# A second GRN product by 38 block products on quarters of the positions in place of 15 on halves

## The chip, the core and the metric

The kernel runs on one core of a Trainium2 chip. The metric is the device time of one execution in microseconds (us). Three runs of the kernel before gave 3122.0, 3122.22 and 3123.13 us; the median is 3122.22. The profile comes from one further execution.

## The reference

The input is 32 images of 384 channels and 28 x 28 = 784 positions, in fp32. A ConvNeXt block with global response normalization is followed by a gate; everything is computed in fp32.

```python
y = depthwise_conv7x7(x) + dw_b                  # per channel
y = layernorm over channels(y) * ln_g + ln_b     # per position
y = gelu(y @ w1 + b1)                            # 384 -> 1536 features
gx = sqrt(sum over positions(y**2))              # per image and feature
y = grn_g * (y * gx / (mean(gx) + eps)) + grn_b + y
x = x + (y @ w2 + b2)                            # 1536 -> 384
avg, mx, mn = mean, max, min of x over the positions
logits = concat(avg @ W1.T, (W2_1 . mx per group) * W2_2, mn @ W3.T) @ Wfc.T
out = sigmoid(logits[:, :, None, None] + x)
```

The change concerns `y @ w2`. For one image it is a product of a 384 x 1536 matrix (the weights) with a 1536 x 784 matrix (the features by positions).

## The kernel before

**Stages.** Until about 484 us the depthwise convolution runs for all images, as matmuls with banded matrices (lines 529 to 533); its result goes to memory (`yd`, `yl`). In the same stretch GpSimd makes the sums of weight blocks that the later products need (`form_w`, lines 448 to 456) and stores them (`u1d`, `u2d`). Then each image has two stages. `up(b)` (line 752) is the first product with GELU, `down(b)` (line 837) the second product with the residual. The order is up(0), up(1), down(0), up(2), down(1), and so on. In mid-run one image takes 81.75 us: for instance a first product starts at 1437.94, the second one at 1477.44 and the next first product at 1519.69 us.

**Both products use a fast block algorithm.** A 3 x 3 by 3 x 2 block product takes 18 block multiplications in the ordinary way. Here it takes 15: each multiplies a sum of weight blocks (made once, ahead) by a sum of input blocks (a "form", made per image), and the results are added to and subtracted from the output blocks. In the second product, the 1536 features are split in three groups by k = 0 to 2 (each of KT = 4 blocks of 128 partitions), and the 784 positions in two halves "a" and "b" of NH = 392. `FORMS` lists the ten sums of inputs, `STEPS` the fifteen products:

```python
    ("s", None, "r", "2a", ALU.subtract),     # FORMS: s = r - 2a
    ("r", "+02-20+21", "B", 0, "+2a"),        # STEPS: input r, weights, bank, first, reads
```

A step loads its summed weights (256 KB, `u2d[i]`, SyncE's DMA queue, six buffers in turn), multiplies four times on TensorE into its bank (line 859; an fp32 matmul is two records in the trace, so a step is eight records of 392 columns), and then VectorE reads the bank into the output `xt`, which holds the residual (lines 873 and 875). An output block and half is read two to four times. The last read of each (line 875) also adds b2 and sums over the positions; once both halves of a block are final, two reductions over 784 positions give its maximum and minimum (line 882).

**The forms** are made by GpSimd, each as one instruction over 4 x 392 = 1568 elements per partition (line 834): seven (`EARLY`) are issued during the preceding first product, three within the second. Six places (`SLOTS`) hold them; some take the place of an input block that is no longer needed. The same ten forms over 392 elements are made for the first product's input (`forms_up`, line 246, instructions of line 269).

**The order around it** is written out by hand as hooks: `within(b)` (line 936) hangs work onto the steps of the first product, `beside(b)` (line 977) onto those of the second. In `within(b)` stand the scaling of the previous image's features by 1 + g * nx (`scale`, line 812, ScalarE), its forms, and half of this image's GELU and squares. In `beside(b)`, where n = b + 1, stand: the transposes of image b+2's normalized input on TensorE and their copies out (`turn`, `evac`), `forms_up(b+2)` at step 4, the input of image b+3 (`load_y`, line 202) at step 3 and its statistics (`stats`, line 208) at step 8, the rest of image n's GELU and squares, its GRN factor (`grn`, line 794), the gate of image b-1 (`gate_store`, line 888) and the load of image n's residual (`load_x`) at step 10. The gate multiplies 96 values of each partition on GpSimd (`zt`, line 894), sums them over partitions by one matmul (`pa`), and so on to the sigmoid.

A framework turns the hooks into one queue per engine; it may move an instruction ahead of others unless the code says `keep_in_program_order`. PSUM has eight banks: seven go round in the pool `psz`, one (`pss`, "small") serves the two tiny matmuls of `grn` and the gate.

Of the kernel before, what the change touches and what calls it, by code (L numbers as in the profile page):

```python
# [56 lines left out]
    ("w", "1b", "0b", "1b", ALU.add),  # L57
# [4 lines left out]
    ("v", None, "u", "2a", ALU.subtract),  # L62
    ("x", "0a", "v", "w", ALU.subtract),
    ("z", "0b", "v", "2b", ALU.subtract),
)
UPFORMS = "pqrstuvwxz"
EARLY = 7
SLOTS = 6

STEPS = (
    ("0b", "+10-11", "G", 1, "-0b+1b"),
    ("0a", "+00", "D", 1, "-1a+0a"),
    ("p", "-20+21", "B", 1, "-2b"),
    ("s", "-02", "E", 1, "+0a"),
    ("r", "+02-20+21", "B", 0, "+2a"),
    ("2a", "-02+20+22", "E", 0, "+2a"),
    ("1a", "+01+20-21", "B", 0, "+0a"),
    ("t", "+00+10-11", "C", 1, "+0b"),  # L80
    ("x", "+20", "A", 1, "+2a"),
    ("u", "-00-10-12", "C", 0, "-1a"),
    ("v", "-12-20", "A", 0, "+1a"),
    ("w", "-11+20", "F", 1, "+1a-1b"),
    ("z", "+12", "A", 0, "-1b"),
    ("q", "+00-01-02+10-11", "B", 0, "-0b"),
    ("2b", "+12+20-21-22", "A", 0, "-2b"),
)
NS = len(STEPS)

# [18 lines left out]
)  # L109
KT = FB // 3  # L110
UG = 5
# [11 lines left out]
def convnext_gate_kernel(  # L123
# [20 lines left out]
    pss = ctx.enter_context(tc.tile_pool(name="pss", bufs=1, space=bass.MemoryType.PSUM))  # L144

    def small(name):
        return pss.tile([P, 512], F32, tag="small", name=name)

# [5 lines left out]
    u2d = dram.tile([NS, P, KT * P], F32, name="u2d")  # L154
# [14 lines left out]
    NQ = 4 * CB  # L169
# [30 lines left out]
    bss = {}  # L200

    def load_y(b):
        yi = yis[b] = yip.tile([P, NY, NJ, YC], F32, tag="yi", name=f"yi_{b}")
        yk = yi.rearrange("p k j c -> p k (j c)")
        nc.sync.dma_start(yk[:, : NY - NLAST], yd[:, :, b, :])
        nc.sync.dma_start(yk[:, NY - NLAST :], yl[:, :, b, :])

    def stats(b):

        mv = sts[b] = smp.tile([P, NJ, 2], F32, tag="mv", name=f"mv_{b}")  # L210
        if b == 0:
            bs = bss[0].rearrange("p j i v -> p j (i v)")
        else:
            bs = smp.tile([P, NJ, 6], F32, tag="bs", name=f"bs_{b}")
            for j in range(NJ):
                nc.vector.bn_stats(bs[:, j, :], yis[b][:, :, j, :])
        for j in range(NJ):
            nc.vector.bn_aggr(mv[:, j, :], bs[:, j, :])

# [26 lines left out]
    def forms_up(b, eng=nc.gpsimd):  # L246
# [6 lines left out]
        if b == 1:  # L253
            aft = [
                dp.tile([P, KT, NH], F32, tag="d", name=f"af_{b}_{i}") for i in range(-(-ns // KT))
            ]
            af = [aft[n // KT][:, n % KT, :] for n in range(ns)]
        else:
            af = [room_af[:, n, :] for n in range(ns)]
        byname = {f[0]: f for f in FORMS}  # L260
        n = 0
        for name in UPFORMS:
            _, place, in0, in1, op = byname[name]
            if name == "w":
# [4 lines left out]
            eng.tensor_tensor(d, o[in0], o[in1], op)  # L269
# [3 lines left out]
    with ExitStack() as one:  # L273
        tp = one.enter_context(tc.tile_pool(name="tp", bufs=1))
        xtp = one.enter_context(tc.tile_pool(name="xtp", bufs=2))
        ufp = one.enter_context(tc.tile_pool(name="ufp", bufs=2))
# [127 lines left out]
        w2v = ws.rearrange("p (t k m c) -> p t k m c", t=KT, k=3, c=P)  # L404
        U1, U2 = 4, 22
        stores = []
        SG = 40

        def gate_weights():

            for h in range(2):
                nc.vector.tensor_scalar(
                    gate[:, : 2 * CB, :].rearrange("p (cb h) r -> p h cb r", h=2)[:, h],
                    awt[:, 0], 1.0 / NT, None, ALU.mult,
                )
            nc.vector.tensor_copy(gate[:, 3 * CB :, :], awt[:, 1])
            for cb in range(CB):
# [10 lines left out]
                out=gate[:, 2 * CB : 3 * CB, :], in_=grp_a, pattern=[[-P, CB], [G, R]],  # L428
                compare_op=ALU.is_ge, fill=0.0, base=G - 1, channel_multiplier=-1,
            )  # L430
            pf = small("pf")
# [5 lines left out]
            for v in range(3):  # L437
                q0, nq = ((0, 2 * CB), (2 * CB, CB), (3 * CB, CB))[v]
# [9 lines left out]
        def form_w(name, wv, text, dst):  # L448

            t = ufp.tile([P, KT, P], F32, tag="uf", name=name)  # L450
# [102 lines left out]
        def store(yc, kt, b0, b1):  # L553
# [6 lines left out]
            if b0 == 0:  # L560
                for j in range(NJ):
                    nc.vector.bn_stats(bss[0][:, j, 1 + i, :], yc[:, 0, j, :])
# [53 lines left out]
        for s in range(NK):  # L616
# [37 lines left out]
            else:  # L654
# [4 lines left out]
                if s % 2:  # L659
                    store(yc, kt, 0, B)  # L660
                    if kt == NY - NLAST - 1:

                        yi = yis[0] = yip.tile([P, NY, NJ, YC], F32, tag="yi", name="yi_0")
                        nc.sync.dma_start(
                            yi[:, : NY - NLAST].rearrange("p k j c -> p k (j c)"), yd[:, :, 0, :]
                        )
                        bs0 = bss[0] = smp.tile(
                            [P, NJ, 1 + NLAST, 6], F32, tag="bs0", name="bs0", bufs=1
                        )
                        for j in range(NJ):  # L670
                            nc.vector.bn_stats(bs0[:, j, 0, :], yi[:, : NY - NLAST, j, :])
# [13 lines left out]
            i = s - U2  # L685
            if 0 <= i < NS:
                form_w(f"u2_{i}", w2v, STEPS[i][1], u2d[i].rearrange("p (t c) -> p t c", c=P))

# [3 lines left out]
    u2_tiles = [up2.tile([P, KT * P], F32, name=f"u2_{i}") for i in range(5)]  # L692
    u2_tiles.append(ws[:, NU1 * UG * P : NU1 * UG * P + KT * P])
# [5 lines left out]
    dp = ctx.enter_context(tc.tile_pool(name="dp", bufs=SLOTS))  # L699
    psz = ctx.enter_context(tc.tile_pool(name="psz", bufs=7, space=bass.MemoryType.PSUM))  # L700
# [93 lines left out]
    def grn(b):  # L794
# [6 lines left out]
        pg = small(f"pg_{b}")  # L801
# [10 lines left out]
    def scale(b, f, eng=nc.scalar):  # L812
        y = ys[b][:, f, :]
        affine(eng, y, y, gscs[b][:, f : f + 1], gb_t[:, f : f + 1])

    def forms(b, n0, n1):
# [248 lines left out]
```

## Time and profile before

| what | value |
|---|---|
| median of three runs | 3122.22 us (3122.0 to 3123.13) |
| profiled execution, its own time | 3123.22 us |
| its span in the trace | 3121.5 us |
| granted TensorE clock, mean | 0.998 |
| ScalarE: GELU (line 744), one of 784 elements | 944 ns, 384 of them |
| VectorE: read of a bank of the first product (line 783), 392 elements | 562 ns |
| VectorE: maximum or minimum over 784 (line 882) | 964 ns, 192 of them |
| GpSimd: form for the first product (line 269), 392 elements | 1015 ns |
| GpSimd: the gate's input (line 894), 96 elements | 350 ns |
| SyncE DMA: weights of the first product, 320 KB | 3.0 us from issue to landing |
| DMA in all | 540.81 MB, mean 173 GB/s |

In a line of the groups, a name such as `pz_A<-y,u` is out<-in with the image's number left out, `128x392 f32` the tile (partitions x elements per partition), `x512` the number of instructions; then follow their busy time in us and the mean of one in ns, and last the idle time of the engine ahead of them with what ended most of it. Durations of matmul records overlap, so their pace is taken from starts. In a line of the timeline, the first number is the start and the second the length of a run of like instructions, both in us, the last `xN` how many there are; `[... <-...]` is the wait ahead of it.

### The profile page before, as it was taken

What the parts mean: (1) busy time and instruction counts of PE and PEld (TensorE: products, weight loads), DVE (VectorE), ACT (ScalarE), POOL (GpSimd) and SP (SyncE); (2) the same over time, 40 slices, a digit from 0 to 9 for tenths busy, and PEclk for the clock granted to TensorE, in tenths of its full rate; (3) what the DMA queues carried; (4) which work ended last, traced back from release to release, by engine and by line L of the source; (5) the groups of instructions that cost most, each with busy time, mean ns of one, the idle gap of its engine ahead of it and who ended that gap; (6) DMA issues with size and microseconds to landing.
All of it is one profiled execution on the core that took longest, in us unless ns stands there. A gap on an engine that the chain in (4) does not pass through costs nothing.

```text
span 3121.5 us, 34685 instructions
## 1 busy us (share of the span) xinstructions
PE 3097.7 (99%) x11555; PEld 2005.6 (64%) x11555; DVE 1683.8 (54%) x3452; ACT 1953.1 (63%) x3123; POOL 1542.5 (49%) x766
## 2 busy tenths in 40 slices
PE   8999999999999999999999999999999999999998
PEld 8999996555555555555555555555555555555554
DVE  3444436655555555555555555555555555555554
ACT  3333335767667677666667666676666766767762
POOL 1232301645555555555555555555555555555555
PEclk9999999999999999999999999999999999999999
DMA  9999976444444444444444444444444444444334
GB/s 366 367 369 352 351 289 202 133 127 133 146 146 144 146 146 144 135 141 146 142 147 142 149 142 150 142 146 145 143 138 138 133 146 147 144 145 146 126 107 130
DMA packets 294315, 540.81 MB, mean 173 GB/s; under 512 B 125151, under 2 KB 134906, under 8 KB 285178
## 3 DMA queue, kind: packets, MB, share of 16 engines
q1 hardware_dynamic: 281156, 499.80, 49.2%
q10 hardware_dynamic: 12982, 38.80, 3.4%
q8 instruction: 93, 1.52, 0.2%
q14 instruction: 84, 0.69, 0.1%
HBM read 447.53 MB, written 90.99 MB: 173 GB/s over the span
## 4 chain that ended last, share of the span: by engine, by line
PE 98%; DMA 1%; ACT 1%; DVE 0%; issue 0%; ACTq 0%; SPq 0%; POOLq 0%; DVEq 0%
PE ph_B L774 13%; PE ph_C L774 13%; PE ph_A L774 13%; PE pz_A L859 11%; PE pz_B L859 11%; PE pz_E L859 5%; PE pz_C L859 5%; PE pc L529 5%; PE pc L533 4%; PE pc L531 4%; PE pz_F L859 3%; PE pz_D L859 3%; PE pz_G L859 3%; PE py L732 2%; PE pt L386 2%; DMA dwb<-in_cvec 0%
## 5 line engine op out<-in xcount | busy, mean ns | idle before, releaser
L744 ACT ACTIVATE y<-y,fv 128x784 f32<-128x784 f32 x384 | 347.2, 944 | 194.3 <-DVE y L789 171.6
L774 PE MATMUL ph_B<-room,ws 128*128 128x392 f32 x1240 | 458.9, 492 | 1.5 <-DMA yi<-yl 1.5
L774 PE MATMUL ph_C<-room,ws 128*128 128x392 f32 x1240 | 459.0, 492 | 0.0
L774 PE MATMUL ph_A<-room,ws 128*128 128x392 f32 x1240 | 458.9, 492 | 0.0
L234 ACT ACTIVATE y<-y,fv,gsc 128x784 f32<-128x784 f32 x376 | 365.5, 1030 | 142.4 <-DVE gsc L810 142.4
L834 POOL TENSOR_TENSOR d_v<-d_u,y 128x1568 f32<-128x1568 f32 x32 | 112.7, 3523 | 588.5 <-PE pz_B L859 588.3
L774 PEld LDWEIGHTS ph_B<-room,ws 128*128 128x128 f32 x1240 | 235.4, 190 | 173.6 <-issue 1.8
L774 PEld LDWEIGHTS ph_A<-room,ws 128*128 128x128 f32 x1240 | 235.5, 190 | 172.8 <-ACT y L781 0.6
L774 PEld LDWEIGHTS ph_C<-room,ws 128*128 128x128 f32 x1240 | 235.3, 190 | 172.2 <-DVE y L787 0.4
L750 ACT ACTIVATE junk<-y 128x784 f32<-128x784 f32 x384 | 328.4, 855 | 6.9
L269 POOL TENSOR_TENSOR room<-room 128x392 f32<-128x392 f32 x300 | 294.3, 1015 | 2.3
L785 DVE TENSOR_TENSOR y<-y,ph_B 128x392 f32<-128x392 f32 x256 | 137.8, 559 | 206.0 <-ACT y L744 129.8
L894 POOL TENSOR_TENSOR zt<-gate,st 128x96 f32<-128x96 f32 x32 | 11.2, 350 | 460.4 <-PE ph_C L774 438.7
L783 DVE TENSOR_TENSOR y<-y,ph_C 128x392 f32<-128x392 f32 x384 | 215.7, 562 | 30.9
L834 POOL TENSOR_TENSOR y<-d_v,y 128x1568 f32<-128x1568 f32 x64 | 223.7, 3517 | 2.4
L545 ACT ACTIVATE yc<-pc,dwb 128x224 f32<-128x224 f32 (+1 forms) x200 | 103.4, 617 | 189.0 <-PE pc L533 180.5
L529 PE MATMUL pc<-xt,tmat 128*128 128x224 f32 (+1 forms) x800 | 213.8, 349 | 4.9 <-ACT xt L397 3.4
L533 PE MATMUL pc<-xt,tmat 128*128 128x192 f32 (+1 forms) x800 | 192.9, 323 | 0.0
L531 PE MATMUL pc<-xt,tmat 128*96 128x192 f32 (+1 forms) x800 | 191.1, 321 | 0.0
L395 DVE COPY xt<-pt 128x512 f32<-128x512 f32 (+1 forms) x184 | 112.0, 618 | 133.7 <-PE pt L386 133.6
L859 PE MATMUL pz_A<-y,u 128*128 128x392 f32 x512 | 179.0, 492 | 0.0
L882 DVE TENSOR_REDUCE st<-x 128x1 f32<-128x784 f32 x192 | 177.1, 964 | 3.3
(168 smaller groups left out, 5701.9 us busy)
## 6 DMA issues: line engine op xcount, KB each, us to landing
ws<-u1d SPq DMA_DIRECT2D x384, 320.0 KB, 3.0
u<-u2d SPq DMA_DIRECT2D x400, 256.0 KB, 2.7
tmat<-fs SPq DMA_DIRECT2D x47, 1420.0 KB, 11.7
yd<-yc SPq DMA_DIRECT2D x22, 1792.0 KB, 6.6
yi<-yd SPq DMA_DIRECT2D x32, 1232.0 KB, 6.9
x<-in_x SPq DMA_DIRECT2D x32, 1176.0 KB, 6.2
out<-x ACTq DMA_DIRECT2D x31, 1176.0 KB, 5.4
room<-in_x SPq DMA_DIRECT2D x84, 392.0 KB, 11.3
```

Of the source, the lines that this page charges most:

```text
L234: eng.activation(out, in_, AF.Identity, bias=add, scale=mul)
L269: eng.tensor_tensor(d, o[in0], o[in1], op)
L529: keep(nc.tensor.matmul(po, t[:, c, P : 2 * P], xc, start=True, stop=False))
L531: nc.tensor.matmul(lo, t[:, c, 2 * P : T0 + MW], after, start=False, stop=False)
L533: keep(nc.tensor.matmul(hi, t[:, c, :P], before, start=False, stop=True))
L744: nc.scalar.activation(y, y, AF.Gelu, bias=b1_t[:, f : f + 1], scale=1.0)
L750: nc.scalar.activation(junk, ys[b][:, f, :], AF.Square, accum_out=ssqs[b][:, f : f + 1])
L774: nc.tensor.matmul(banks[t, bk][:, :NH], wts[t][:, i % UG, :], o[opnd], start=(first == 1), stop=True, skip_group_check=True,)
L783: nc.vector.tensor_tensor(d, d, p, ALU.add)
L834: nc.gpsimd.tensor_tensor(d, o[in0], o[in1], op)
L859: nc.tensor.matmul(pz[:, :NH], wt[:, t, :], o[opnd][:, t, :], start=(first == 1 and t == 0), stop=(t == KT - 1), skip_group_check=True,)
L882: nc.vector.tensor_reduce(st[:, q : q + 1], xt[:, m, :], AX.X, op2)
```

## The change

The second product becomes a 4 x 3 by 4 x 4 block product: the features are split in four groups (KD = 3 blocks of 128 each), the weights' outputs in three as before, the positions in four quarters "a" to "d" of NQ4 = 196. In the ordinary way that is 48 block products; the new `STEPS` have 38, and `SUMS` has 39 sums of inputs of 3 x 196 = 588 elements per partition, some of which only serve further sums. A step is three matmuls of 196 columns. With it come:

- **Sums by need** (`sums(b)`, `used(b, name)`): GpSimd's sums are issued in the fixed order of `SUMS`, each as soon as its inputs are scaled and a place is free. There are 15 places of 588 elements; a place is freed after the last use, counted in program order. The call stands after every step and in the hooks of the first product. `forms_up` is issued when all sums are ("after sums").
- **Weights**: two steps' weights per load (`UD` = 2, 384 KB, 19 loads per image), five buffers. There are 38 weight sums to be made during the convolution, with 109 terms in place of 36.
- **Reads**: 51 in place of 18, of 196 columns. Twelve are final ones; each of these now has its own maximum and minimum over 196 positions at once, and three small reductions at the end join the quarters.
- **Order**: the features are scaled in the group order 1, 3, 2, 0, six blocks still in the second product and six in the first. The input of image b+1 is loaded at the start of up(b), with its issue behind the last weight load of the second product (`issue_after`); its statistics go into the second half of up(b)'s first pass (hooks (0, 20) to (0, 28)) one block at a time. The input of image 0 is loaded in two parts.
- **Banks**: the pool of the small matmuls is gone, `psz` has eight.
- **The end**: the gate of image b-1 hangs at step `part(11)` = 27 of down(b) in mid-run, at `part(9)` = 22 in down(30) and at step ND - 8 = 30 in down(31), the last one; the last image's sums are offered at every step of down(30) from `part(8)` = 20 on.

```diff
--- before.py
+++ after.py
-UPFORMS = "pqrstuvwxz"
-EARLY = 7
-SLOTS = 6
...
+SUMS = (
+    ("s0", "1b", "+", "1c"),
+    ("s1", "3c", "-", "2c"),
+    ("s2", "s0", "+", "s1"),
+    ("s3", "s2", "+", "3d"),
+    ("s4", "3c", "-", "s2"),
...
+    ("s38", "2d", "+", "s5"),
+)
+STEPS = (
+    ("s3", "+13+21", "A", "+1a+1d"),
+    ("s4", "-11+13", "B", "+1c"),
+    ("s8", "+11+12+21", "C", "-1a-1c"),
+    ("s9", "-13", "D", "+1a"),
...
+    ("s38", "+12", "C", "+1d"),
+    ("2b", "-02-03-12-13-22-23", "F", "-1b"),
+)
+SCALED = (1, 3, 2, 0)
+ND = len(STEPS)
+KD = FB // 4
+NQ4 = NT // 4
+SLOTS = 15
+UD = 2
+TURNED = 10
...
-    pss = ctx.enter_context(tc.tile_pool(name="pss", bufs=1, space=bass.MemoryType.PSUM))
-    def small(name):
-        return pss.tile([P, 512], F32, tag="small", name=name)
     fs = [dram.tile([P + 1, FL], F32, name=f"fs_{cb}") for cb in range(CB)]
     NY = C // YC
     yd = dram.tile([P, NY - NLAST, B, NJ * YC], F32, name="yd")
     u1d = dram.tile([KT, P, NS, P], F32, name="u1d")
-    u2d = dram.tile([NS, P, KT * P], F32, name="u2d")
+    u2d = dram.tile([ND // UD, P, UD * KD * P], F32, name="u2d")
...
-    NQ = 4 * CB
+    NQ = 3 * CB
...
-        nc.sync.dma_start(yk[:, : NY - NLAST], yd[:, :, b, :])
+        with tc.issue_after(last_u2[-1]) if last_u2 else ExitStack():
+            nc.sync.dma_start(yk[:, : NY - NLAST], yd[:, :, b, :])
...
-            bs = smp.tile([P, NJ, 6], F32, tag="bs", name=f"bs_{b}")
-            for j in range(NJ):
-                nc.vector.bn_stats(bs[:, j, :], yis[b][:, :, j, :])
+            bs = bss.pop(b)
...
+    def block_stats(b, j):
+        if j == 0:
+            bss[b] = smp.tile([P, NJ, 6], F32, tag="bs", name=f"bs_{b}", bufs=2)
+        nc.vector.bn_stats(bss[b][:, j, :], yis[b][:, :, j, :])
...
         if b == 1:
+            n = -(-ns * NH // (KD * NQ4))
+            reserved.extend(slots[SLOTS - n :])
+            del slots[SLOTS - n :]
+            aft = d_room[:, (SLOTS - n) * KD * NQ4 :]
+            af = [aft[:, n * NH : (n + 1) * NH] for n in range(ns)]
...
+            tc.keep_in_program_order(eng.tensor_tensor(d, o[in0], o[in1], op))
...
-            i = s - U2
-            if 0 <= i < NS:
-                form_w(f"u2_{i}", w2v, STEPS[i][1], u2d[i].rearrange("p (t c) -> p t c", c=P))
+            for i in range(ND):
+                if s != U2 + i * (NK - 2 - U2) // ND:
+                    continue
+                form_w(
+                    f"u2_{i}", w2v, STEPS[i][1],
+                    u2d[i // UD].rearrange("p (u t c) -> p u t c", u=UD, c=P)[:, i % UD],
+                )
...
+    NU2 = 5
+    u2_tiles = [up2.tile([P, UD * KD * P], F32, name=f"u2_{i}") for i in range(NU2 - 1)]
+    u2_tiles.append(ws[:, NU1 * UG * P :])
     tep = ctx.enter_context(tc.tile_pool(name="tep", bufs=2))
     ynp = ctx.enter_context(tc.tile_pool(name="ynp", bufs=3))
     junkp = ctx.enter_context(tc.tile_pool(name="junkp", bufs=1))
     yp = ctx.enter_context(tc.tile_pool(name="yp", bufs=2))
     xp = ctx.enter_context(tc.tile_pool(name="xp", bufs=2))
-    dp = ctx.enter_context(tc.tile_pool(name="dp", bufs=SLOTS))
-    psz = ctx.enter_context(tc.tile_pool(name="psz", bufs=7, space=bass.MemoryType.PSUM))
+    dp = ctx.enter_context(tc.tile_pool(name="dp", bufs=1))
+    d_room = dp.tile([P, SLOTS * KD * NQ4], F32, name="d_room")
+    all_slots = [
+        d_room[:, i * KD * NQ4 : (i + 1) * KD * NQ4].rearrange("p (t n) -> p t n", n=NQ4)
+        for i in range(SLOTS)
+    ]
+    slots, reserved = list(all_slots), []
+    psz = ctx.enter_context(tc.tile_pool(name="psz", bufs=8, space=bass.MemoryType.PSUM))
...
-        pg = small(f"pg_{b}")
+        pg = bank(f"pg_{b}")
...
+    def sums(b):
+        if b not in ops:
+            yv = ys[b].rearrange("p (t k) n -> p t k n", k=4)
+            o = {
+                f"{k}{'abcd'[q]}": (yv[:, :, k, q * NQ4 : (q + 1) * NQ4], False)
+                for k in range(4)
+                for q in range(4)
+            }
+            spare = []
+            if b == B - 1:
+                n = KD * NQ4
+                spare = [
+                    room[:, i * n : (i + 1) * n].rearrange("p (t n) -> p t n", n=NQ4)
+                    for i in range(room.shape[1] // n)
+                ]
+            ops[b] = o, dict(USES), spare, list(SUMS)
+        o, uses, spare, todo = ops[b]
+        while todo:
+            name, a, sign, c = todo[0]
+            if any(x[0] != "s" and scaled.get((b, int(x[0])), 0) < KD for x in (a, c)):
+                return
+            if slots:
+                d = slots.pop(0), True
+            elif spare:
+                d = spare.pop(0), False
             else:
-                d = o[place]
-            nc.gpsimd.tensor_tensor(d, o[in0], o[in1], op)
+                alone = [x for x in (a, c) if uses[x] == 1]
+                if not alone:
+                    return
+                d = o[alone[0]]
+                uses[alone[0]] += 1
+            todo.pop(0)
+            tc.keep_in_program_order(
+                nc.gpsimd.tensor_tensor(
+                    d[0], o[a][0], o[c][0], ALU.add if sign == "+" else ALU.subtract
+                )
+            )
             o[name] = d
+            for x in (a, c):
+                used(b, x)
+    def used(b, name):
+        o, uses, spare, _ = ops[b]
+        uses[name] -= 1
+        if uses[name] == 0:
+            place, shared = o[name]
+            (slots if shared else spare).append(place)
...
     def down(b, hooks):
...
+        stq = smp.tile([P, 3, CB, 4], F32, tag="stq", name=f"stq_{b}")
...
+            if i % UD == 0:
+                wt = u2_tiles[(b * (ND // UD) + i // UD) % NU2]
+                last_u2.append(nc.sync.dma_start(wt, u2d[i // UD]).ins)
+                wt = wt.rearrange("p (u t c) -> p u t c", u=UD, c=P)
...
+                    pz[:, :NQ4],
+                    wt[:, i % UD, t, :],
+                    o[opnd][0][:, t, :],
+                    start=(first and t == 0),
+                    stop=(t == KD - 1),
...
+            used(b, opnd)
             for sg, m, hn in terms(reads):
-                h = "ab".index(hn)
-                xh = xt[:, m, h * NH : (h + 1) * NH]
+                h = "abcd".index(hn)
+                xh = xt[:, m, h * NQ4 : (h + 1) * NQ4]
                 op = ALU.add if sg > 0 else ALU.subtract
                 left[m, hn] -= 1
                 if left[m, hn]:
-                    nc.vector.tensor_tensor(xh, xh, pz[:, :NH], op)
+                    nc.vector.tensor_tensor(xh, xh, pz[:, :NQ4], op)
                     continue
                 nc.vector.scalar_tensor_tensor(
-                    xh, xh, b2_t[:, m : m + 1], pz[:, :NH], ALU.add, op,
-                    accum_out=st[:, 2 * m + h : 2 * m + h + 1],
+                    xh, xh, b2_t[:, m : m + 1], pz[:, :NQ4], ALU.add, op,
+                    accum_out=stq[:, 0, m, h : h + 1],
                 )
-                if not left[m, "ab"[1 - h]]:
-                    for v, op2 in ((2, ALU.max), (3, ALU.min)):
-                        q = v * CB + m
-                        nc.vector.tensor_reduce(st[:, q : q + 1], xt[:, m, :], AX.X, op2)
+                for v, op2 in ((1, ALU.max), (2, ALU.min)):
+                    nc.vector.tensor_reduce(stq[:, v, m, h : h + 1], xh, AX.X, op2)
+            sums(b)
+            if pending and not todo and i > TURNED:
+                run(hooks, "after sums")
+                pending = False
             run(hooks, i)
+        assert not pending
+        for v, op2 in enumerate((ALU.add, ALU.max, ALU.min)):
+            nc.vector.tensor_reduce(st[:, v * CB : (v + 1) * CB], stq[:, v], AX.X, op2)
...
-    order = [f for f in range(FB) if f % 3] + [f for f in range(FB) if f % 3 == 0]
+    order = [4 * t + k for k in SCALED for t in range(KD)]
...
         else:
+            for i, f in enumerate(order[HF:]):
+                at((0, 5 + 2 * i), scale, p, f)
+            for i in range(0, 13, 6):
+                at((0, 4 + i), sums, p)
...
+        if 2 <= b and b + 1 < B:
+            at((0, 0), load_y, b + 1)
+            for j in range(NJ):
+                at((0, 20 + j), block_stats, b + 1, j)
+            at((0, 28), stats, b + 1)
+            at((0, 28), std, b + 1)
...
     def beside(b):
...
+        def part(i):
+            return i * ND // 15
...
+            for i, jj in ((0, (0, 1)), (3, (2, 3)), (7, (4, 5)), (TURNED, (6,))):
                 for j in jj:
                     at(i, turn, b + 2, j)
-                for j in ((3, 4), (5, 6))[i] if i < 2 else ():
+                for j in {0: (3, 4), 3: (5, 6)}.get(i, ()):
                     at(i, norm, b + 2, j)
-                if i in (1, 4):
-                    at(i, evac, b + 2, i // 4)
-            at(4, forms_up, b + 2)
-        if b + 3 < B:
-            at(3, load_y, b + 3)
+                if i in (3, TURNED):
+                    at(i, evac, b + 2, i // TURNED)
+            at("after sums", forms_up, b + 2)
...
-            at(10, gate_store, b - 1)
+            at(part(11) if n < B else ND - 8, gate_store, b - 1)
-            at(10 if b else 0, load_x, n)
+            at(part(11) if b else 0, load_x, n)
             for i, f in enumerate(order):
-                at(4 + i // 3, scale, n, f)
-            at(8, forms, n, 0, 4)
-            at(9, forms, n, 4, EARLY)
+                at(part(4 + i // 3), scale, n, f)
+            for i in range(part(8), ND):
+                at(i, sums, n)
             if b >= 1:
+                at(part(9), gate_store, b - 1)
+        elif n < B:
+            for i, f in enumerate(order[:HF]):
+                at(part(9) + 1 + i, scale, n, f)
```

## The prediction

> **What bounds the kernel now.** I read the page from the top: busy times, then the chain that ended last, then the groups.
>
> ```profile
> PE 3097.7 (99%) x11555; PEld 2005.6 (64%) x11555; DVE 1683.8 (54%) x3452; ACT 1953.1 (63%) x3123; POOL 1542.5 (49%) x766
> ...
> PE 98%; DMA 1%; ACT 1%; DVE 0%; issue 0%; ACTq 0%; SPq 0%; POOLq 0%; DVEq 0%
> ```
>
> TensorE is busy 99% of the span and 98% of the chain; the next engine, ScalarE, has 63%. A busy TensorE need not be a fast one, since a matmul's profiled duration (492 ns for 392 columns) overlaps its neighbour's. What counts is the distance between starts, which the timeline gives: first the second product in mid-run, then the convolution, whose matmuls have the width that the change brings.
>
> ```profile
> 1499.82 1.15 PE L859 MATMUL pz_C<-d_t,u 128*128 128x392 f32 x3
> 1500.81 2.80 PE L859 MATMUL pz_A<-y,ws 128*128 128x392 f32 x8
> 1503.44 0.82 PE L859 MATMUL pz_C<-d_u,u 128*128 128x392 f32 x2
> ```
> ```profile
> 301.34 0.49 PE L531 MATMUL pc<-xt,tmat 128*96 128x192 f32 x2
> 301.67 0.49 PE L533 MATMUL pc<-xt,tmat 128*128 128x192 f32 x2
> ```
>
> Eight records of 392 columns take 1503.44 - 1500.81 = 2.63 us, 0.329 us each, with no gap. An fp32 matmul is two such records. 192 columns take (301.67 - 301.34)/2 = 0.1625 us by the finer start times. The line through both is 2.5 ns + 0.833 ns per column. So TensorE's column count is the bound, and the change must be summed on it first.
>
> **The second product (TensorE).** Before, an image has 15 steps x 4 matmuls x 2 = 120 records of 392 columns: 120 x 0.329 = 39.50 us. After, 38 x 3 x 2 = 228 records of 196 columns: 2.5 + 196 x 0.833 = 165.8 ns, 37.81 us. That is 1.69 us less per image, 54.1 us for 32 images. All of it lies on the bound.
>
> [...]
>
> ```profile
> L774 PEld LDWEIGHTS ph_B<-room,ws 128*128 128x128 f32 x1240 | 235.4, 190 | 173.6 <-issue 1.8
> ```
>
> 190 ns is more than 165.8. If loads followed each other at 190 ns, they would set the pace and the change would lose. [...] The trace decides for the shorter one: line 533 loads 128 columns of weights for 192 moving ones and keeps 163 ns, and where only 96 columns move (480 us) the pace is about 112 ns, not the 82 ns of the line above. So a load occupies some 0.11 us, and 190 ns is a latency. [...]
>
> **The sums (GpSimd).** Removed: 10 forms per image. Added: 39 sums of 588 elements.
>
> ```profile
> 1486.97 3.53 POOL L834 TENSOR_TENSOR d_v<-d_u,y 128x1568 f32<-128x1568 f32 x1 [19.37 <-PE pz_B L859]
> 1490.58 6.99 POOL L834 TENSOR_TENSOR y<-d_v,y 128x1568 f32<-128x1568 f32 x2
> 1497.52 9.89 POOL L269 TENSOR_TENSOR room<-room 128x392 f32<-128x392 f32 x10
> ```
>
> 1568 elements take 3.52 us from start to start, 392 take 0.988. Interpolated, 588 take 0.988 + 196 x 2.15 ns = 1.41 us (bounds 1.38 and 1.55, the latter if each waits for the one before). 39 x 1.41 = 55.0 us instead of 35.2, and with the 9.9 us of the first product's forms and the 0.35 us of the gate GpSimd has 65 us of work in a period of 80. Whether it is in time I worked out from the built program's queue order, with t = 0 at the start of a second product (40.3 us with its transposes), preceded by 39.5 us of first product. Sums s2 to s24 queue behind the previous image's gate input, which VectorE finishes about 3 us into the first product: 3 + 23 x 1.41 = 35.5, so s24 is there before t = 0, and step 16 needs it at t = 18. s25 to s30 wait for places that steps 1 to 9 free; step 9 ends at t = 12, nine sums then take 12.7, the ten forms 9.9, done at 34.6; the next first product asks at 40.3. So GpSimd is hidden, with 5.7 us to spare; the time per sum could rise to 2.0 us.
>
> **VectorE.** A read of 392 columns takes 0.48 us start to start (1.04 us for two with the last one's latency), i.e. 0.408 of data and 0.07 fixed; no row shows 196 columns, so it costs between 0.275 (the slope) and 0.48 (no gain); I take 0.275, as 784-element reductions (0.89) lie on the same line. Reads go from 18 to 51. Of these, 12 are final ones with two reductions each, about 1.0 us a group, bunched in steps 25 to 37: 12.1 us, and 2 us of others, in 12.9 us. VectorE ends the second product about 1.5 us behind; then come the statistics of the next input (3.4 us), moved here from the second product. Its first sub-result is wanted at 7.9 us of the first product, and I find it at 7.3. Hidden, by 0.6 us. If a piece costs 0.05 us more, 36 late pieces give 1.8 us, and TensorE waits 1.2 us per image; below nothing this cannot go, since TensorE waits for no read now.
>
> **Weights.** 19 loads of 384 KB replace 15 of 256 KB, one per 1.99 us: 198 GB/s during the second product.
>
> ```profile
> u<-u2d SPq DMA_DIRECT2D x400, 256.0 KB, 2.7
> ```
>
> 320 KB land in 3.0 us, so 384 in about 3.4; a buffer is reloaded four pairs (8 us) ahead. The input load moves behind the last weight load in SP's queue, and the x load stands at the stage's end, so no weights queue behind 1.2 MB. Cost nothing; if the cover were gone, 3.4 - 1.99 = 1.4 us per load. The 38 weight sums in the convolution (109 terms of about 1.0 us against 36) take some 115 us of GpSimd's mostly idle 240; their stores are 31 GB/s against 26: nothing, at most 3 us.
>
> **Both ends.** Image 0 has only nine places until the first product of image 1 ends: its chain ends near 624 us, and the third first product asks for its ninth form at 621: +2 us (0 to 5). At the end, image 31's sums can't start before image 30's are through (22.7 us after the start of image 30's second product); 39 x 1.41 + 0.35 brings GpSimd to 78.1, and image 30's gate product stands in TensorE's queue after step 30 of image 31, behind all of them. Seven steps follow: end at 85.2 instead of 76.0, +9.2 us (8 to 15). The tail gets shorter by 1.2 us (two reductions of 784 become 196).
>
> **Sum.** -54.1 + 2 + 9.2 - 1.2 = -44.1 us, on the profiled execution's 3123.2 us (span 3121.5): 3079.1. The median of the runs lies 1.0 below it: 3078 us.
>
> **The rivals.** (1) VectorE late: the 0.6 us is misjudged, and 0.3 to 1.3 us per image come back as waits of the first matmuls of each first product for banks or sub-results: 3087 to 3118, say 3100. For it: twelve groups in thirteen steps. Against: no such wait now, and 28 + 4 us of VectorE work in 39.5 us of first product. (2) GpSimd late in mid-run: a sum costs over 2.0 us, because VectorE and GpSimd disturb each other; at 2.2 us, 39 x 2.2 + 10.2 = 96 us a period would be far slower, at 2.05 some 0.5 us per image: 3094. Against: 3.52 us holds in both stages of the trace. (3) Slower: the weight load sets the pace of the 196-column records. Its place is every record of the second product; at 190 ns it is 43.3 us per image, +3.8 x 32 + 10 = +132: 3254. It decides from 39.50/228 = 173 ns. Against: line 533. (4) That fewer columns are not multiplied is ruled out: the program holds 3648 matmuls of 196 columns against 1920 of 392.
>
> **Chances.** Forecast (3066 to 3092) 0.67; rival 1 0.18; rival 2 0.06; rival 3 0.05; a better result than 3066 (ends cost nothing) 0.04. The range 3066 to 3106 leaves out the last, rival 3, and the upper parts of 1 and 2, together under 0.2. Within 0.2% (6 us), about what a measurement can tell from no change, lie the edges of rivals 1 and 2, 0.04; slower 0.06; faster 0.90.
>
> **What would show it.** TensorE's second-product records start 166 ns apart; sums of 588 elements near 1.41 us; stalls in mid-run near zero; the last gate product waiting for GpSimd some 3 us and steps of the last image waiting for sums; GpSimd near 76%, VectorE near 60%. It is wrong if the pace is 173 ns or more, or if waits on VectorE or weights recur with each image.

## The result and the profile after

The changed kernel takes 3095.85 us, the median of four runs (3092.25 to 3095.95), against 3122.61 us before. The ratio is 0.9912 with a 95% interval of 0.9894 to 0.9929. The gain is 27 us where 44 were forecast. The time lies inside the range of 3066 to 3106, but above the forecast's own 3066 to 3092 and in the territory of rival 1. The profiled execution took 3095.95 us, its span is 3094.2 us.

The busy times and the chain that ended last, after:

```profile
PE 3059.3 (99%) x15011; PEld 2486.7 (80%) x15011; DVE 1986.1 (64%) x5378; ACT 1986.7 (64%) x3151; POOL 2263.1 (73%) x1767
...
PE 95%; POOL 3%; ACT 1%; DVE 1%; DMA 1%; issue 0%; ACTq 0%; SPq 0%; POOLq 0%; DVEq 0%
```

TensorE is still the bound, but GpSimd now holds 3% of the chain. The second product in mid-run, from TensorE's timeline:

```profile
1562.99 1.16 PE L980 MATMUL pz_A<-d_room,u 128*128 128x196 f32 x6
1563.99 0.49 PE L816 MATMUL py<-ident,yn 128*128 128x128 f32 x3
```

Six records take 1563.99 - 1562.99 = 1.00 us. The median distance of all 7296 records of this form is 166.0 ns; 165.8 were forecast, and 173 was the break-even. The other sizes, from the groups and the DMA issues:

```profile
L941 POOL TENSOR_TENSOR d_room<-d_room,y 128x588 f32<-128x588 f32 x309 | 442.5, 1436 | 16.8
...
u<-u2d SPq DMA_DIRECT2D x487, 384.0 KB, 3.4
```

VectorE's reads, from its timeline, two in a row and one alone:

```profile
605.00 0.63 DVE L995 TENSOR_TENSOR x<-x,pz_C 128x196 f32<-128x196 f32 x2 [0.37 <-PE pz_C L980]
...
606.99 0.36 DVE L995 TENSOR_TENSOR x<-x,pz_G 128x196 f32<-128x196 f32 x1 [0.37 <-PE pz_G L980]
```

In mid-run a sum takes 1.42 us from start to start in the first product and 1.51 us beside the second one (medians; forecast 1.41), a load lands in 3.4 us (forecast 3.4), and a read of 196 columns follows another by 0.63 - 0.36 = 0.27 us (forecast 0.275).

So the durations were right. To find the lost 17 us I cut the run at the starts of second products and compared the stretches:

| stretch | before | after | change |
|---|---|---|---|
| start to the third second product | 741.70 us | 747.75 us | +6.05 |
| the next 28 images | 2288.97 (81.749 each) | 2249.09 (80.325 each) | -39.88 |
| from the second product of image 30 to the end | 90.84 | 97.36 | +6.52 |

Per image 1.69 us were to be gained, 32 times. In mid-run 1.42 arrived. At the start two images' worth (3.4 us) and 6.05 more were lost, 9.4 in all; at the end likewise 3.4 + 6.5 = 9.9. To place each loss I took the distances between starts of neighbouring records and subtracted the median of their form; what is left are TensorE's waits.

**Mid-run.** In each image three gaps of 66, 97 and 103 ns stand 13 to 15 us behind the start of the first product, and none at its start, where rival 1 had put them. The timelines there, ScalarE first, then VectorE, GpSimd and TensorE's weight loads (PEld):

```profile
1521.38 0.50 ACT L865 ACTIVATE te<-ph_A 128x392 f32<-128x392 f32 x1 [1.57 <-PE ph_A L858]
1522.63 0.71 ACT L308 ACTIVATE yn<-yi,nmr,rstd 128x384 f32<-128x384 f32 x1 [0.75 <-DVE nmr L301]
1523.24 0.48 ACT L865 ACTIVATE te<-ph_A 128x392 f32<-128x392 f32 x1
1523.62 1.29 ACT L308 ACTIVATE yn<-yi,nmr,rstd 128x384 f32<-128x384 f32 x2
1524.82 0.86 ACT L865 ACTIVATE y<-ph_A 128x392 f32<-128x392 f32 x2
```
```profile
1521.20 0.19 DVE L299 RECIPROCAL rstd<-sd 128x7 f32<-128x7 f32 x1
1521.43 1.17 DVE L301 SCALAR_TENSOR_TENSOR nmr<-mv,rstd 128x7 f32<-128x7 f32 x1
...
1525.33 1.04 DVE L871 TENSOR_TENSOR y<-ph_C,y 128x392 f32<-128x392 f32 x2 [1.01 <-ACT y L865]
```
```profile
1521.15 1.42 POOL L941 TENSOR_TENSOR d_room<-d_room,y 128x588 f32<-128x588 f32 x1
```
```profile
1523.77 0.30 PEld L858 LDWEIGHTS ph_A<-room,ws 128*128 128x128 f32 x2 [0.43 <-ACT te L865]
...
1525.95 0.30 PEld L858 LDWEIGHTS ph_C<-room,ws 128*128 128x128 f32 x2 [0.56 <-DVE y L871]
```

Between two copies of banks (`te<-ph_A`) ScalarE has a normalization of the next image, and it stands 0.75 us until VectorE has `nmr`. The second copy is late, and TensorE waits for its bank (the first gap). Two more normalizations (1523.62) stand ahead of the next copies; a read of VectorE waits 1.01 us for these, and TensorE for the read (the other two gaps). And `nmr`, seven elements, takes 1.17 us: it ends at 1522.60, just behind GpSimd's sum (1521.15 + 1.42 = 1522.57).

**Start.** TensorE waits 4.0 us between 598 and 610 us, in image 0's second product, nearly all for sums of GpSimd; then it runs slowly for 3.4 us:

```profile
609.88 1.92 PE L980 MATMUL pz_H<-d_room,u 128*128 128x196 f32 x6 [1.51 <-POOL d_room L941]
611.59 2.17 PE L980 MATMUL pz_A<-d_room,u 128*128 128x196 f32 x6
613.55 1.26 PE L980 MATMUL pz_C<-d_room,u 128*128 128x196 f32 x6
```

The step from 611.59 to 613.55 lasts 1.96 us instead of 1.00. In the table by stretches, where the third number from the end is the granted clock:

```profile
600.00:608.00 8.00, 7.71 (x42) 6.81 (x43) 3.22 (x10) 0.00 (x0) 7.92 (x6) 1.00 0.48 144
609.90:613.50 3.60, 3.60 (x12) 3.60 (x13) 1.34 (x1) 2.23 (x3) 3.44 (x3) 0.56 0.19 30
614.00:620.00 6.00, 6.00 (x38) 6.00 (x38) 4.83 (x21) 6.00 (x8) 5.69 (x5) 1.00 0.61 180
```

The clock is 0.56 there and 1.00 on both sides; by this TensorE falls 1.7 us behind. Yet this is not a cost of its own. The third first product then waits for its ninth form, which GpSimd makes behind all the sums. First the changed kernel, then `pin_norm` (experiment 1), where the same waits of 4.0 us for sums stand but the clock stays at 1.00:

```profile
629.73 1.58 PE L858 MATMUL ph_A<-room,ws 128*128 128x392 f32 x4 [0.35 <-POOL room L343]
```
```profile
626.63 1.58 PE L859 MATMUL ph_A<-room,ws 128*128 128x392 f32 x4 [1.99 <-POOL room L342]
```

By the distances of records these gaps are 0.51 and 2.16 us: what the half clock does not take, the wait for the form takes. The form comes 133.7 us after the start of image 0's first product (629.73 - 496.04) and 133.4 in `pin_norm` (626.63 - 493.25), so GpSimd's chain of sums and forms sets the loss: 4.0 + 1.7 + 0.5 = 6.2 us. With 1.0 us ahead of 568.1 (VectorE's sub-results behind four scalings) and 0.6 + 0.3 us in the first products of images 2 and 3 (the normalizations, as in mid-run) this makes 8.1 of the 9.4 us. The other 1.3 lie in small gaps; 0.3 of it is already there when image 0's first product starts (495.73 us before, 496.04 after).

**End.** In the last image TensorE waits 8.9 us, spread over steps 5 to 16 (counted from 0), and again a half clock comes with it (granted 0.50 from 3059.5 to 3063 us):

```profile
3055.36 1.26 PE L980 MATMUL pz_F<-room,u 128*128 128x196 f32 x6 [0.91 <-POOL room L941]
3059.52 2.33 PE L980 MATMUL pz_E<-y,u 128*128 128x196 f32 x6 [2.90 <-POOL y L941]
3061.64 2.17 PE L980 MATMUL pz_D<-y,u 128*128 128x196 f32 x6
```

Behind the wait of 2.90 us the steps take 2.1 us: 2.2 us more. Here too GpSimd's chain decides. The gate product of image 30 stands behind step 30 of image 31; first the changed kernel, then `pin_norm`, where the half clock lasts 3.4 us in place of 6.8:

```profile
3076.99 0.37 PE L1023 MATMUL pa<-zt,ones_f 128*128 128x72 f32 x2
```
```profile
3065.41 0.44 PE L1024 MATMUL pa<-zt,ones_f 128*128 128x72 f32 x2 [0.25 <-POOL zt L1022]
```

It starts 80.15 and 80.10 us after image 30's second product (2996.84 and 2985.31), each time right behind GpSimd's last instruction for it (80.03 and 80.05), and the stretch to the end of the run takes 97.36 and 97.39 us. With less half clock TensorE waits for GpSimd at the gate product instead.

### The profile page after: what moved, and what is told of

The parts are those of the page before. It is cut to its first block, busy times and chain, and to the rows that moved or that the text cites. A ratio compares the mean times of both kernels' runs of the same rounds, so it can differ in the third digit from the quotient of the medians.

```text
span 3094.2 us, 45727 instructions
## 1 busy us (share of the span) xinstructions
PE 3059.3 (99%) x15011; PEld 2486.7 (80%) x15011; DVE 1986.1 (64%) x5378; ACT 1986.7 (64%) x3151; POOL 2263.1 (73%) x1767
## 4 chain that ended last, share of the span: by engine, by line
PE 95%; POOL 3%; ACT 1%; DVE 1%; DMA 1%; issue 0%; ACTq 0%; SPq 0%; POOLq 0%; DVEq 0%
PE ph_A L858 13%; PE ph_C L858 13%; PE ph_B L858 13%; PE pz_A L980 8%; PE pz_C L980 8%; PE pz_D L980 7%; PE pz_F L980 7%; PE pc L599 5%; PE pc L603 4%; PE pc L601 4%; PE py L816 2%; PE pt L460 2%; PE pz_H L980 2%; PE pz_E L980 2%; PE pz_I L980 2%; POOL d_room L941 1%
## 5 line engine op out<-in xcount | busy, mean ns | idle before, releaser
L941 POOL TENSOR_TENSOR d_room<-y 128x588 f32<-128x588 f32 x257 | 368.2, 1439 | 342.4 <-PE pz_B L980 194.0
L941 POOL TENSOR_TENSOR d_room<-d_room,y 128x588 f32<-128x588 f32 x309 | 442.5, 1436 | 16.8
L941 POOL TENSOR_TENSOR d_room<-y,d_room 128x588 f32<-128x588 f32 x220 | 316.0, 1437 | 46.0 <-PE pz_A L980 18.2
L941 POOL TENSOR_TENSOR y<-y 128x588 f32<-128x588 f32 x188 | 269.7, 1435 | 7.3
L867 DVE TENSOR_TENSOR y<-y,ph_C 128x392 f32<-128x392 f32 x384 | 214.3, 559 | 27.4
L1002 DVE TENSOR_REDUCE stq<-x 128x1 f32<-128x196 f32 x768 | 228.2, 349 | 5.5
L980 PE MATMUL pz_A<-d_room,u 128*128 128x196 f32 x1056 | 204.9, 330 | 0.0
L524 POOL TENSOR_SCALAR u<-ws 128x384 f32<-128x384 f32 (+1 forms) x53 | 66.5, 1259 | 186.7 <-DMA u2d<-u 133.8
## 6 DMA issues: line engine op xcount, KB each, us to landing
tmat<-fs SPq DMA_DIRECT2D x47, 1420.0 KB, 11.4
```

What stands on the lines that cost most here:

```text
L867: nc.vector.tensor_tensor(d, d, p, ALU.add)
L941: nc.gpsimd.tensor_tensor(d[0], o[a][0], o[c][0], ALU.add if sign == "+" else ALU.subtract)
L980: nc.tensor.matmul(pz[:, :NQ4], wt[:, i % UD, t, :], o[opnd][0][:, t, :], start=(first and t == 0), stop=(t == KD - 1), skip_group_check=True,
L1002: nc.vector.tensor_reduce(stq[:, v, m, h : h + 1], xh, AX.X, op2)
```

## The experiments

The theory was threefold: mid-run, ScalarE's queue (the normalization ahead of a bank copy); start and end, GpSimd's rate. The rival: VectorE has too much to do. The edits for these three were made alone and together; the later ones stand on top of the first.

**1. The normalizations pinned** (`pin_norm`):

```diff
-                at((2, 24 + 2 * j), norm, b + 1, j)
+                at((2, 24 + 2 * j), norm, b + 1, j, A, True)
...
+        if pin:
+            tc.keep_in_program_order(ins)
```

> The three normalizations of the next image (ScalarE) keep their place in program order, behind the copies of banks that the framework had let them overtake. VectorE's and GpSimd's work is unchanged. Theory (ScalarE stands in the normalization and waits for nmr, so its copies of the banks come late and TensorE waits 0.27 us in each first product): the gaps between records of the first product fall from 8.3 us in mid-run to about 1, the time from 3095.9 to about 3089. Rival (VectorE has too much work in the first product, as rival 1 of the prediction had it): the gaps stay, 3095 to 3097.

3086.07 us (3084.41 to 3087.67), ratio to before 0.9885 (0.9871 to 0.9898): 9.8 us below the changed kernel. In mid-run the gaps of the first product fell from 8.3 to 0.6 us, and an image takes 80.06 us, 1.69 less than before. The groups, first of the changed kernel, then of this one:

```profile
L308 ACT ACTIVATE yn<-yi,nmr,rstd 128x384 f32<-128x384 f32 x210 | 137.6, 695 | 23.6 <-DVE nmr L301 22.9 <-DMA ws<-u1d 0.7
```
```profile
L307 ACT ACTIVATE yn<-yi,nmr,rstd 128x384 f32<-128x384 f32 x210 | 136.8, 692 | 0.0
```

ScalarE's 22.9 us of waiting for `nmr` are gone. `nmr` itself is as slow as before the edit (1092 ns), so VectorE's amount of work is not what cost the time; with ScalarE's order put right, a late `nmr` costs nothing. Whether a quick `nmr` in the old order would have done as well was not tried. The gain in mid-run is 7.4 us. Of the other 4.1 us between the two profiled executions, 0.9 are the normalizations of the first products of images 2 and 3, and 2.8 lie ahead of image 0's first product (496.04 against 493.25 us), which the edit does not touch; the half clock at 610 us, which this execution did not show, counts for nothing (see Start).

**2. Sums on VectorE** for the last image (`last_share`), the first (`first_share`), and both with the pinning (`all_three`):

```diff
-                nc.gpsimd.tensor_tensor(
+                (nc.vector if b == B - 1 and n % 3 == 2 else nc.gpsimd).tensor_tensor(
```

> Every third of the last image's 39 sums (13) is made by VectorE instead of GpSimd. Theory (the last image's products wait for GpSimd's rate, 1.38 us a sum against 1.0 us a step, and one wait of 2.9 us then halves TensorE's clock for 4 us): the 13.6 us of gaps at the end fall to 3 to 5, time 3086 to 3088. If VectorE's sums and GpSimd's exclude each other at the memory (VectorE's small two-input instructions seem to wait for GpSimd's to end), 26 x 1.4 + 13 x 0.7 = 45.5 us of the two together instead of 54.6: still enough, near 3088. Rival (the end is set by the reads or the gate): no change, 3095 to 3097.

> Of the first image's sums 16 to 38, every third (8 sums) is made by VectorE. Theory (from 598 to 610 us the second product waits for GpSimd's sums, 4.0 us, and then runs 3.6 us at half clock, 1.8 us): these gaps go, time 3090 to 3092. Rival (places, not GpSimd's time, are what is short with nine places: a sum waits for a place that a later step frees): most of the gaps stay, 3094 to 3096.

> The three edits together. If the three causes are apart, the gains add: 7 + 9 + 5 = 21 us, about 3075 (3072 to 3080). If VectorE's late work is behind them all, less than half of that.

All three missed, with the sign wrong: 3116.54, 3106.26 and 3118.98 us, which is 21, 10 and 23 us above the changed kernel. VectorE's timeline in the last image of `last_share`, then GpSimd's:

```profile
3024.39 0.76 DVE L942 TENSOR_TENSOR d_room<-y 128x588 f32<-128x588 f32 x1
...
3025.90 0.37 DVE L1033 TENSOR_REDUCE lg<-lt 128x3 f32<-128x216 f32 x1
3030.76 1.97 DVE L942 TENSOR_TENSOR room<-d_room 128x588 f32<-128x588 f32 x1 [4.49 <-POOL d_room L942]
3032.65 2.00 DVE L942 TENSOR_TENSOR room<-d_room,y 128x588 f32<-128x588 f32 x1
```
```profile
3030.68 1.42 POOL L942 TENSOR_TENSOR room<-d_room,y 128x588 f32<-128x588 f32 x1
3032.06 1.96 POOL L942 TENSOR_TENSOR room<-y 128x588 f32<-128x588 f32 x1
3033.99 1.94 POOL L942 TENSOR_TENSOR d_room<-y 128x588 f32<-128x588 f32 x1
```

VectorE stands 4.49 us for a sum of GpSimd that its own next sum needs, then makes four sums in a row in 7.6 us, and its reads of the banks stand behind them: TensorE then waited 10.7 us for one read. In `first_share` it waited 9.46 us in the same way. Besides, two sums side by side take 1.97 and 1.95 us instead of 0.76 and 1.42, so that GpSimd's own share gets slower too. The edit put GpSimd's lateness into VectorE's queue. These runs do not speak against GpSimd as the cause at both ends; they show that VectorE is not its relief in this order of queues. `all_three` keeps the gain in mid-run (gaps of 0.6 us) beside both losses: the causes are apart.

**3. Places for the last sums** (`room_30`, on top of the pinning): image 30 may use the room of the first product's forms.

```diff
-            ops[b] = o, dict(USES), spare, list(SUMS)
+            ops[b] = o, dict(USES), last_spare if b == B - 1 else [], list(SUMS)
...
+        if b == B - 2:
+            n = KD * NQ4
+            af = CB * NT
+            for w in (af + 2 * NH, af + 6 * NH, af + 6 * NH + n, 0, n, 2 * n, 3 * n, af, af + 4 * NH):
+                last_spare.append(room[:, w : w + n].rearrange("p (t n) -> p t n", n=NQ4))
```

> On top of the pinned normalizations: the last sums of image 30 may take places in the room of the first product's forms, which no later image needs, instead of waiting for places that its own steps free. Theory (at the end GpSimd starts the last image's sums late because it stood 7.3 us waiting for places in the image before, and TensorE then waits for GpSimd): the last image's sums come up to 7 us earlier, the waits of TensorE in the last image fall from 11 us to 3 to 6, its half-clock stretch (about 2 us) goes, time 3086.1 - 7 to 9 = 3077 to 3079. Rival (the end is bound by VectorE's reads or the gate chain): 3085 to 3087.

3085.01 us: one microsecond, where 7 to 9 were expected. GpSimd no longer waits for places, but for something else, as its timeline shows:

```profile
3003.73 1.44 POOL L934 TENSOR_TENSOR d_room<-y 128x588 f32<-128x588 f32 x1 [1.65 <-ACT y L307]
3009.32 1.44 POOL L934 TENSOR_TENSOR d_room<-y 128x588 f32<-128x588 f32 x1 [4.16 <-ACT y L307]
```

It stands 5.8 us for ScalarE's scaling of the last image. The wait had only been behind the other one.

**4. The gate behind the last step** (`end_gate`) **and a third of the scalings on VectorE** (`end_all`), each on top of the one before:

```diff
-            at(part(11) if n < B else ND - 8, gate_store, b - 1)
+            at(part(11) if n < B else ND - 1, gate_store, b - 1)
...
-                at(part(4 + i // 3), scale, n, f)
+                at(part(4 + i // 3), scale, n, f, V if i % 3 == 2 else A)
```

> On top of the places in the forms' room: the gate product of image 30 stands behind all steps of the last image in TensorE's queue, not behind step 30. Theory (there TensorE waited 2.29 us for GpSimd, which makes the gate's input after its last sum): that wait goes, time 3085.0 - 2.3 = 3082.7 (3082 to 3084), unless the gate of the last image, which follows on VectorE and ScalarE, then ends later by the 2.6 us of image 30's sigmoid on ScalarE: 3085.

> In addition, every third of the last image's scalings (4 of 12) is made by VectorE. Theory (with the places given, GpSimd stands 5.8 us waiting for ScalarE's twelve scalings of the last image, 11.3 us in a row): nine scalings are ready 3 us earlier, the sums too, and the waits of TensorE in the last image (1.9, 1.7, 1.8 us) fall by 3 to 5 us: 3078 to 3080. Rival (VectorE's scalings of 784 elements wait for GpSimd's instructions and delay its reads): no gain, 3082 to 3085.

3084.30 us (3082.88 to 3086.62) and 3082.47 us (3080.55 to 3083.64). The sizes are near the scatter of the runs, so the traces decide. From the second product of image 30 on TensorE's gaps are 11.7 us in `room_30`, 9.5 in `end_gate` and 6.6 in `end_all`; but the whole stretch to the end of the run takes 95.6, 96.1 and 93.2 us. In `end_gate` the wait at the gate product goes, and as much is lost behind the last step: from its last matmul to the end the run takes 13.4 us instead of 10.4. This is the exception that the expectation named, but only 0.7 us of it are ScalarE's sigmoids; the rest lies behind them, at the stores. Image 30's output lands at 3080.98 instead of 3073.16, and the last image's three stores beside it take 4.8 us instead of 2.5. `end_all` then gains 2.9 us in the stretch, a little less than the 3 to 5 forecast; its time of 3082.47 lies in the range of its rival (no gain, 3082 to 3085), but TensorE's waits fell as the theory had it. `end_all` is the fastest of the kernels: its ratio to before is 0.987 (0.9854 to 0.9887), 40 us.

**5. GpSimd's spare time** (`late3`, `late7`, on top of the pinning): three or seven of the late sums of images 1 to 30 are made twice.

```diff
...
+            twice = 1 <= b < B - 1 and free and name in ['s33', 's34', 's35']
+            for _ in range(2 if twice else 1):
```

> On top of the pinned normalizations: in images 1 to 30 the sums s33 to s35 are computed twice over (the same values again), 3 x 1.4 = 4.2 us more of GpSimd's time late in the second product. Theory (GpSimd is done with the ten forms at 36.4 us of the second product, and the ninth form is first wanted at 42.9, so 6 to 7 us are spare): no change, 3085 to 3088. Rival (no spare: GpSimd is at its limit): 29 x 4 = 116 us more, 3200.

> As before with seven sums twice over (s30, s33 to s38), 7 x 1.4 = 9.9 us more. Theory (spare of 6 to 7 us): 2 to 4 us of wait per image, perhaps with half-clock stretches behind them: 29 x 2 to 4 = 60 to 120 us more, 3145 to 3205. If the spare is over 10 us: no change.

`late3` took 3090.48 us, 4.4 more than `pin_norm`, where no change was expected. Mid-run is unchanged at 80.06 us an image (0.6 us of gaps in all first products together), so 4.2 us are free there. The loss is at the end, which the theory had left out: image 31 begins later (18.0 us of gaps against 13.5). `late7` took 3215.95 us, over the 3145 to 3205 expected: 118 us in 29 images, as expected, and 10 more at the end. TensorE's timeline:

```profile
1633.01 1.48 PE L859 MATMUL ph_C<-room,ws 128*128 128x392 f32 x4
1637.22 2.53 PE L859 MATMUL ph_A<-room,ws 128*128 128x392 f32 x4 [2.73 <-POOL room L342]
1639.54 2.27 PE L859 MATMUL ph_B<-room,ws 128*128 128x392 f32 x4
```

The first product's third step waits for the ninth form, 2.9 us in each image: of 9.9 us added, 7.0 were spare. And in 19 of 29 images the half clock follows, for 3.4 us (in the image shown, granted 0.50 from 1637.7 to 1640.0 us): with it an image takes 84.7 us, without it 83.0, so it costs 1.7 us each time, and the mean cost of an image is 4.1 us.

**6. Weights for one product at a time** (`one_load`, on top of the pinning): `UD = 1`, ten buffers of half the size.

> On top of the pinned normalizations: the weights of the second product come for one step at a time, 38 loads of 192 KB with ten buffers of half the size (the same memory). Theory (the weights are hidden, 8 us ahead): no change, 3084 to 3088. Rival (a load of half the size takes nearly as long to land, so that the smaller packets and 19 more issues make the queue the bound): TensorE waits for weights in each second product, over 3100.

3086.24 us against 3086.07: no difference. The two-step load is not what the change lives on.

## Why the prediction came out as it did

| term of the sum | forecast | measured |
|---|---|---|
| pace, 32 images | -54.1 | 1.690 us an image with the normalizations pinned: -54.1 |
| waits in mid-run | 0 | (80.325 - 80.059) x 28 = +7.4 |
| start | +2 (0 to 5) | +9.4, of it 6.2 by GpSimd's chain |
| end with its tail | +9.2 - 1.2 = +8.0 | +9.9 |
| sum | -44.1 | -27.4 (span: 3121.5 to 3094.2, -27.3) |

- **Pace: right**, and with it the choice of 165.8 ns over the 190 ns of the weight loads' row. The loads still show 190 ns each, while records follow each other at 166.0 ns. Rival 3 falls: the 190 ns did not set the pace.
- **Sums in mid-run: right.** Forms done at 36.4 us of the second product (forecast 34.6). By `late7` 7 us were to spare (forecast 5.7, up to the start of the next first product); the ninth form is wanted only by its third step. Sums cost 0.1 us more beside the second product than in the interpolation (1.51 against 1.41 us).
- **Weights: right**, no wait for them, and `one_load` shows that their form doesn't matter.
- **VectorE in mid-run: the step failed, not by its amount.** "Hidden, by 0.6 us" held at the place it was made for, the first sub-results. But "then come the statistics of the next input (3.4 us), moved here" was costed as VectorE's time alone. What counted was who waits for their result: ScalarE's normalization, which the framework put ahead of a bank copy. I followed the moved step to VectorE, but not `nmr` on to the engine that waits for it. Rival 1's price (0.3 to 1.3 us per image) just missed the measured 0.27, and its mechanism, VectorE late for banks and sub-results at the start of the first product, did not occur. That the time lies in the range is in part luck: the part above 3092 had been drawn for rival 1, and what took the time there was ScalarE's order (7.4 us), the start (7.4 over its forecast) and the end (1.9 over).
- **Start: mis-sized.** The +2 stood for the wait of the third first product for its ninth form, and there the loss is settled, at 6.2 us. The term that was too small is GpSimd's chain: it was to end near 624 us and ended at 630.65. After its first sum it stood 2.7 us for ScalarE, the 38 others followed each other by 1.47 us instead of 1.41 (2.2 us), and the forms took 10.4 us instead of 9.9. I left out that TensorE meets most of this lateness in image 0's own steps, which want their sums one after the other (4.0 us), and put at nothing VectorE's scalings in front of sub-results (1.0) and the normalizations (0.9).
- **End: the path right, the size a little short.** GpSimd's chain, the gate product of image 30 right behind it and seven steps make the end, as forecast: GpSimd was done at 80.0 us after the start of image 30's second product (forecast 78.1), and this lateness is nearly all that is over. Where TensorE waits was wrong: not some 3 us at the gate product (nothing in the changed kernel, 0.4 us in `pin_norm`), but in earlier steps, each for its sum.
- **The tail** ends sooner than before from the last matmul on, 10.1 us against 11.4, as forecast (1.2).

What stays open: the 1.3 us of small gaps at the start, and how to shorten GpSimd's chain in image 0, for which the only edit tried (`first_share`) made it worse.

## What to carry to other kernels

When a step moves, follow its result to the instruction that waits for it, and look what stands behind that instruction in its engine's queue: 0.75 us of ScalarE's waiting and two more instructions ahead of bank copies cost 0.27 us per image and 7.4 us in all, and fixing the order of three instructions brought them back. A steady state that fits with room to spare says nothing of the first and the last image, where the same engine begins late: add up that engine's own chain, with its waits, to its last result. TensorE's waits on the way there, and a half clock behind them, only shifted the same loss here: with 6.8 us of half clock in the last image and with 3.4 the run's last stretch took 97.36 and 97.39 us. And relief for a late engine must not bring its waits into the queue of an engine that others depend on.

## What the runs showed of the hardware

**VectorE's small instructions beside GpSimd.** In the changed kernel `nmr`, seven elements from two input tiles, took 1178 ns (median) where it fell into a sum of GpSimd, and 158 ns elsewhere. Groups of before, then after:

```profile
L227 DVE SCALAR_TENSOR_TENSOR nmr<-mv,rstd 128x7 f32<-128x7 f32 x32 | 6.0, 187 | 0.1
```
```profile
L301 DVE SCALAR_TENSOR_TENSOR nmr<-mv,rstd 128x7 f32<-128x7 f32 x32 | 34.8, 1088 | 1.0
```

Of the 32 after, 29 fell into a sum, and all 29 ended 19 to 32 ns after the end of a sum; the three others took 156 to 159 ns. The last step of the GRN factor (line 894, twelve elements, one input tile) looks the same: 940 ns where it fell into a form or a sum, each time ending 28 to 34 ns behind one, and 161 and 174 ns in the two other cases. A reciprocal (line 299) took 193 ns inside a sum, which then ran on for about 1.2 us, and 193 to 202 in the other cases: no such wait is seen there. Before, `nmr` as a rule began 936 ns into a form of 1015 ns and took 159 ns, so it hardly showed: 3 of the 32 took 384 to 592 ns. Why one instruction ends with GpSimd's and the other does not, these traces don't show; they show that `nmr` took 1.0 us longer.

**The half clock.** Apart from the run's beginning and end, the changed kernel's trace has a granted clock of 0.5 twice: for 3.4 us from 610.3 us on, behind 4.0 us of waits between 598 and 610 us, and for 6.8 us from 3057.7 us on, beginning within the wait of 2.90 us. `pin_norm` had the same 4.0 us of waits in image 0 and kept 1.00. In `late7` the 29 waits are alike, 2.9 us each; 19 of them were followed by a half clock and 10 were not. One of the 19, where the third number from the end is the granted clock (the wait in the first line, what follows it in the second):

```profile
1634.50:1637.10 2.60, 0.00 (x0) 0.00 (x0) 2.17 (x5) 1.42 (x2) 2.52 (x3) 1.00 0.17 63
1637.70:1640.00 2.30, 2.30 (x5) 1.24 (x4) 0.00 (x0) 0.71 (x2) 2.30 (x3) 0.50 0.86 240
```

So like waits were followed by a half clock in some images and not in others, and what decides between the two is not shown. What it cost is: 1.7 us for each of the 19 images of `late7` (84.7 against 83.0 us). In image 0 of the changed kernel it cost nothing of its own, since TensorE then had the less to wait for the ninth form: 0.51 us, against 2.16 in `pin_norm`.
